# Attention and LoRA block on one core: queries of 23 of 32 pairs by seven products of halves, block transfers over three issuing queues, masks of the expert map built later

## The chip, the cores and the metric

The kernel runs on one core of a Trainium2 chip. A core has a matrix engine (PE, with its weight loads shown as PEld), a vector engine (DVE), a scalar engine (ACT), a general engine (POOL) and a queue engine that only issues transfers (SP). All work on a shared on-chip memory (SBUF); PE writes into a small accumulation memory (PSUM) of eight banks, which DVE and ACT can read. Transfers are issued by SP, ACT or POOL and wait in the issuing engine's own order. The metric is the device time of one execution in microseconds, as the median of several runs.

## The reference

The input x has 1024 rows of 512 features, in float32 throughout. With LN for a layer norm without weights, the block computes

```
h   = LN(x)
q   = h @ w_q   (32 heads of 128)      k, v = h @ w_k, h @ w_v   (8 heads of 128)
a   = softmax(causal(q k^T / sqrt(128))) v         four query heads share one k, v head
x   = x + LN(a @ w_o)
h   = LN(x)
y   = h @ base_W^T + base_b + 2 * sum_e (h A_e^T * weight_e) B_e^T
out = x + LN(y)
```

The weights of the experts come from a router: a softmax over 15 logits, the top eight of them, and `expert_map`, which says to which of eight experts each of the 15 belongs.

## The kernel before

The 1024 rows are eight tiles of 128 rows, t = 0 to 7. A group g is one of the eight k, v heads with its four query heads. A **block** is one (g, t): the attention of 128 rows for four heads. Two blocks with neighbouring t form a **pair** (g, u), whose queries are projected together, 256 rows at a time. There are 64 blocks and 32 pairs; groups 0 to 5 run one after the other with t rising, groups 6 and 7 are interleaved at the end, in pairs, and there the second half (router, base product, LoRA) follows each finished tile.

A loop over the blocks (`for i in range(N)`, L804) issues everything. In each block i four **score** steps run, each for 32 rows of all four heads (L403): PE multiplies the queries with all keys up to there (one or two matmuls of at most 512 columns, with the queries as weights), DVE adds the causal mask and takes the maximum (L420, L422), ACT takes the exponential with its sum (L427), and a step later ACT divides by the sum (L434) and DVE transposes 32 x 32 squares into the tile T (L440). POOL clears the part of the row behind the diagonal (`memset`, L425). Two score tiles in PSUM alternate. When T is full, sixteen transfers (`to_keys`, L452) move its 32-row squares to their places in the tile K, which is what the next product needs. K and T have one buffer each for even and for odd t.

Between the scores, `run_share` spreads the rest of the block's PE work over its four quarters by column count. That work is a list, made anew for every block:

- in odd blocks `q`, the query projection of the next pair (`project_q`, L330): four heads, each a sum over four chunks of 128 features, 16 matmuls of 256 columns; two heads share a PSUM bank and ACT copies each bank out, scaled by 1/sqrt(128) (L343);
- `pv`, the product of v and K for the block two earlier (`weighted_values`, tile `po`, L462), t + 1 matmuls of 512 columns; ACT copies its result to `attnT` (L468);
- in even blocks `o_pair`, the output projection of a pair four blocks back (`project_o_pair`, L510). It is already done by seven products of halves: sums of the operands (`sums`, on DVE, L519 to L522; of the weights on POOL, `combine_o`, L505), products pa to pf, and accumulations by DVE (L543);
- projections of k and v, and later the router and the base product.

The order is `then = begins[:1] + q + ends[:-1] + rest[:4] + ...` (L821): in an odd block all the queries come first and the weighted values after them. A float32 matmul runs as two passes on PE, each with its own weight load, so the trace has two rows for each.

What is kept in program order and what is not: instructions wrapped in `keep` stay in written order on their engine; the others are placed by a scheduler. Matmuls, transfers and most score work are kept. PSUM has four banks for the two score tiles, three for a rotating tag `pm` that all projections share, and one for `po`. The query weights of a group, two tiles of 512 KB, have one buffer each and are loaded by ACT's queue at the start of the last but one block of the group before (`load_q`, L120, L724).

For blocks 3 to 62, `to_keys` issues all sixteen transfers from SP (`alone`, L447); for the first three and the last, two of three come from SP and the third from POOL. At block 8 `prepare_ffn` (L199) lets POOL load the second half's small weights and the expert map, and DVE turns the map into eight masks (L208 to L214), which the router uses from block 55 on or so.

Of the kernel before, what the change touches and what calls it, by code (L numbers as in the profile page):

```python
# [15 lines left out]
P = 128  # L16
# [6 lines left out]
def kernel(  # L23
# [28 lines left out]

    nc = tc.nc
    S, H = x.shape
    D = P
# [30 lines left out]
    blocks = [(g, 2 * u + e) for g, u in pairs for e in range(2)]  # L88
    N = len(blocks)
    N2 = (G - 2) * NT  # L90

    def keep(ins):
        return tc.keep_in_program_order(ins)
# [11 lines left out]
    def load(dst, src, by=nc.sync):  # L105
        keep(by.dma_start(dst, src))  # L106
# [13 lines left out]
    def load_q(g, i, by=nc.scalar):  # L120

        if weights.get(("q", i), (None,))[0] == g:
            return
        hw = R * D // 2
        w = wp.tile([P, KC, hw], F32, tag=f"wq{i}", name=f"wq_{g}_{i}", bufs=1)
        load(w, w_q[:, ts(2 * g + i, hw)].rearrange("(c p) n -> p c n", p=P), by)
        weights["q", i] = (g, w)

    def load_v(gv, i, by=nc.scalar):

# [66 lines left out]
            keep(nc.vector.tensor_copy(smask[ts(h, SQ), :], mask[ts(h, SQ), ts(h, SQ)]))  # L197

    def prepare_ffn():  # L199

        load(ra_sb[:, :, :NR], router_wt.rearrange("(c p) n -> p c n", p=P), nc.gpsimd)
        load(ra_sb[:, :, NR:], a_t.rearrange("(c p) n -> p c n", p=P), nc.gpsimd)
        load(bt_sb, b_t, nc.gpsimd)
        load(bias_bc, base_b.partition_broadcast(P), nc.gpsimd)
        load(rb_bc, router_b.partition_broadcast(P), nc.gpsimd)
        load(emap_i, expert_map.partition_broadcast(P), nc.gpsimd)
        emap_f = const.tile([P, NR], F32, tag="emap_f", name="emap_f")
# [110 lines left out]
    def project_k(g, qb):  # L318
        def finish(pm):
            kT = kTs[g, qb] = act.tile([P, QB], F32, tag="kT", name=f"kT_{g}_{qb}", bufs=2 * NQB)  # L320
            nc.scalar.copy(kT, pm)

        def term(c):
            return weights["k", g][:, c, :], xnT[qb][:, c, :]

        return chained(
            lambda: bank(f"pk_{g}_{qb}"), [lambda c=c: term(c) for c in range(KC)], finish
        )

    def project_q(g, u):  # L330

        pm = {}

        def get(j):
            if j % 2 == 0:
                pm[0] = bank(f"pq_{g}_{u}_{j}")
            return pm[0][:, ts(j % 2, PQ)]

        def finish(j):
            if j == 0:  # L340
                qTs[g, u] = act.tile([P, PQ // SQ, R, SQ], F32, tag="qT", name=f"qT_{g}_{u}")
            if j % 2:
                nc.scalar.mul(  # L343
                    qTs[g, u][:, :, j - 1 : j + 1, :].rearrange("p s h q -> p h s q"),
                    pm[0].rearrange("p (h s q) -> p h s q", h=2, q=SQ),
                    scale,
                )

        def term(j, c):
            w = weights["q", j // 2]  # L350
            assert w[0] == g
            rhs = xnT[u * PQ // QB][:, c, ts(u % (QB // PQ), PQ)]
            return w[1][:, c, ts(j % 2, D)], rhs
# [9 lines left out]
        return work  # L363

    turned, keyed = {}, {}

# [36 lines left out]
    def scores(g, t, j):  # L403

        n = t * P + (j + 1) * SQ
        full = (t + 1) * P
        name = f"{g}_{t}_{j}"
        s = ps_s.tile([P, S], F32, tag="s", name=f"s_{name}")
        for c0 in range(0, n, QB):
            w = min(QB, n - c0)  # L410
            matmul(
                s[:, c0 : c0 + w],
                qTs[g, t // 2][:, (t % 2) * NSUB + j, :, :].rearrange("p h q -> p (h q)"),
                kTs[g, c0 // QB][:, :w],
                start=True,
                stop=True,
            )
# [12 lines left out]

        def rescale():
            rec = small.tile([P, 1], F32, tag="rec", name=f"rec_{name}")
            keep(nc.vector.reciprocal(rec, total))  # L433
            keep(nc.scalar.mul(p[:, :n], p[:, :n], rec))  # L434

        def finish():
            if j == 0:
                turned[g, t] = turn_view(turn_tile("T", g, t), t)
            pin(
                nc.vector.transpose(  # L440
                    turned[g, t][:, :, j, :, :].rearrange("p b k q -> p k b q"),
                    p[:, :full].rearrange("p (k b q) -> p k b q", b=R, q=SQ),
                )
            )
            if j == NSUB - 1:
                three = (nc.sync, nc.sync, nc.gpsimd)
                alone = 3 <= blocks.index((g, t)) < N - 1  # L447
                to_keys(g, t, by=three[:1] if alone else three)

        score_tile["rescale"], score_tile["finish"] = rescale, finish  # L450

    def to_keys(g, t, by=(nc.sync,)):  # L452

        src = turned.pop((g, t))
        dst = keyed[g, t] = turn_view(turn_tile("K", g, t), t)
        for h in range(R):
            for b in range(NSUB):
                load(dst[ts(b, SQ), h], src[ts(h, SQ), b], by[(h * NSUB + b) % len(by)])
# [227 lines left out]
    def projections(i):  # L686


        g, t = blocks[i]
        q, other = [], []  # L690
        m = i // 2 + 1
        if i == 0:
            later["q"] = project_q(*pairs[m])
            q = later["q"][: 2 * KC]
        elif i == 1:
            q = later["q"][2 * KC :]
        elif i % 2 and m < len(pairs):
            q = project_q(*pairs[m])
        if i < N2:
            if t == 2:  # L700
                other += project_k(g, 1)
            if t == 6:
                other += project_k(g + 1, 0)
            if g == 0 and t < 2:
                other += [(P * KC, lambda n=TPB + 2 + t: input_turn(n))]
                other += project_v(0, 2 + t)
            elif g % GV == 0 and (g or t >= TPB):
                other += project_v(g // GV, t)
        else:
# [94 lines left out]
    for i in range(N):  # L804
# [13 lines left out]
            begins = ffn_router(t)  # L818

        rest = o + weave(o_pair, other + pv[:2] + begins[1:] + pv[2:])  # L820
        then = begins[:1] + q + ends[:-1] + rest[:4] + ends[-1:] + rest[4:]  # L821
        for n in range(NSUB):
            scores(*blocks[i], n)
            run_share(then, n, NSUB)
        if i == 1:
            combine_o(0)
        if i == NT:
            prepare_ffn()
        ready += complete(i, 7, 8)
        for t in [t for t in ready if ("done", t) in state]:  # L830
            ready.remove(t)
# [81 lines left out]
```

## Time and profile before

| what | value |
|---|---|
| three runs | 1087.78, 1087.92, 1088.68 us (median 1087.92) |
| the profiled execution | 1087.64 us |
| its span, first to last instruction | 1085.9 us |
| mean granted PE clock | 0.996 |
| busy: PE, PEld, DVE, ACT, POOL | 98%, 65%, 60%, 45%, 11% |
| query projection on PE | 1024 rows |
| transfers K<-T | 1004 from SP, 20 from POOL |

A row of the profile reads: line of the kernel, engine, operation, tile written <- tiles read, shape, count; then busy time, mean duration of one in ns, and idle time of the engine before it with what ended that. Matmuls overlap in the pipeline, so the distance between starts tells their pace and not their duration. In a timeline row the first number is the start and the second the length of what was merged, in microseconds from the start of the span. Tile names carry no buffer numbers: `pq` is the PSUM tile of the queries, `s` a score tile, `po` that of the weighted values.

### The profile page before, as it was taken

Reading aid. Unit: us, or ns where it says so; the run is one execution under the profiler, and the core shown is the slowest. Engines: PE = TensorE matmul, PEld = TensorE weight load, DVE = VectorE, ACT = ScalarE, POOL = GpSimd, SP = SyncE. Lnnn points to the kernel's source line nnn. Section 1 sums busy time; section 2 is a strip of 40 time slices with the busy share of each in tenths; the row PEclk is TensorE's granted clock in tenths of the full one; section 3 lists DMA queues with packets and bytes.
Section 4 is the critical chain, followed back from the end, with each engine's and each line's share of the span. In section 5 each row is a group of like instructions: output and inputs, shape, how many; then the busy total and the mean of one; then the engine's idle time right before and its main releaser. Section 6 shows DMA issues by size and latency. Waiting matters only on the chain.

```text
span 1085.9 us, 12864 instructions
## 1 busy us (share of the span) xinstructions
PE 1068.1 (98%) x3846; PEld 705.7 (65%) x3846; DVE 652.6 (60%) x1528; ACT 492.3 (45%) x992; POOL 115.0 (11%) x300
## 2 busy tenths in 40 slices
PE   8999999999999999999999999999999999999986
PEld 7776666666676666666676666666777566466443
DVE  4566546665465555765456555665346766576747
ACT  2654535554345434544345444555335554453511
POOL 2500012000110002000020001100020110111212
PEclk9999999999999999999999999999999999999998
DMA  5244352554135432455125441464333755544221
GB/s 184 62 107 124 68 119 63 160 137 92 36 71 158 92 85 52 121 140 117 39 65 142 103 108 42 105 169 115 88 104 101 170 132 124 131 104 103 71 78 39
DMA packets 79061, 111.82 MB, mean 103 GB/s; under 512 B 18176, under 2 KB 50560, under 8 KB 78992
## 3 DMA queue, kind: packets, MB, share of 16 engines
q1 hardware_dynamic: 52976, 82.08, 32.0%
q10 hardware_dynamic: 25040, 27.27, 7.9%
q0 software_dynamic: 976, 1.65, 0.7%
q8 instruction: 31, 0.51, 0.2%
q14 instruction: 38, 0.31, 0.1%
HBM read 33.34 MB, written 2.10 MB: 33 GB/s over the span
## 4 chain that ended last, share of the span: by engine, by line
PE 87%; DVE 5%; ACT 2%; DMA 2%; SPq 1%; POOL 1%; issue 1%; POOLq 0%; ACTq 0%; DVEq 0%
PE po L100 21%; PE s L100 19%; PE pq L100 18%; PE pk L100 5%; PE pv L100 4%; PE pe L100 4%; PE pa L100 4%; PE pO L100 2%; PE pc L100 2%; PE pb L100 2%; PE pd L100 2%; PE pf L100 2%; DVE T L440 1%; SPq L106 1%; DVE nmax L422 1%; ACT p L427 1%
## 5 line engine op out<-in xcount | busy, mean ns | idle before, releaser
L100 PE MATMUL po<-K,v 128*128 128x512 f32 x576 | 277.4, 596 | 6.2 <-DMA K<-T 4.6
L100 PE MATMUL s<-kT,qT 128*128 128x512 f32 (+15 forms) x768 | 271.8, 463 | 0.0
L427 ACT ACTIVATE p<-s,nmax 128x32 f32<-128x32 f32 (+31 forms) x256 | 179.2, 700 | 198.3 <-DVE nmax L422 192.2
L434 ACT ACTIVATE p<-p,rec 128x32 f32<-128x32 f32 (+31 forms) x256 | 187.9, 734 | 178.1 <-DVE rec L433 121.2
L440 DVE STREAM_TRANSPOSE T<-p 128x128 f32<-128x128 f32 (+7 forms) x256 | 198.4, 775 | 103.1 <-ACT p L434 88.9
L100 PE MATMUL pq<-xnT,wq 128*128 128x256 f32 x1024 | 235.7, 379 | 0.0
L100 PEld LDWEIGHTS s<-kT,qT 128*128 128x128 f32 x768 | 145.6, 190 | 122.1 <-issue 108.1
L100 PEld LDWEIGHTS pq<-xnT,wq 128*128 128x128 f32 x1024 | 192.8, 190 | 38.5 <-issue 16.5
L422 DVE TENSOR_REDUCE nmax<-s 128x1 f32<-128x32 f32 (+31 forms) x256 | 180.7, 706 | 8.3
L100 PEld LDWEIGHTS po<-K,v 128*128 128x128 f32 x576 | 107.7, 191 | 80.3 <-issue 63.8
L420 DVE TENSOR_TENSOR s<-s,smask 128x32 f32<-128x32 f32 x256 | 47.6, 186 | 124.9 <-PE s L100 124.3
L425 POOL MEMSET p<- 128x96 f32 (+2 forms) x192 | 29.8, 156 | 842.7 <-DVE T L440 775.4
L433 DVE RECIPROCAL rec<-total 128x1 f32<-128x1 f32 x256 | 39.8, 155 | 51.9 <-ACT p L427 49.7
L100 PE MATMUL pv<-wv,xnT 128*128 128x256 f32 x256 | 67.3, 380 | 0.4 <-ACT xnT L255 0.4
L343 ACT ACTIVATE qT<-pq 128x512 f32<-128x512 f32 x64 | 38.1, 595 | 65.3 <-PE pq L100 65.2
L468 ACT COPY attnT<-po 128x512 f32<-128x512 f32 x64 | 37.3, 583 | 61.5 <-PE po L100 61.3
L100 PE MATMUL pk<-xnT,wk 128*128 128x512 f32 x128 | 64.5, 593 | 0.0
L100 PE MATMUL pa<-wo,attnT 128*128 128x256 f32 x224 | 62.7, 390 | 0.0
L100 PEld LDWEIGHTS pa<-wo,attnT 128*128 128x128 f32 x224 | 41.8, 193 | 19.8 <-issue 14.8
L100 PEld LDWEIGHTS pv<-wv,xnT 128*128 128x128 f32 x256 | 48.0, 190 | 9.9 <-issue 2.7
L427 ACT ACTIVATION_READ_ACCUMULATOR p<-s,nmax 128x1 f32 x256 | 49.5, 193 | 0.0
L519 DVE TENSOR_TENSOR sums<-attnT 128x256 f32<-128x256 f32 x28 | 11.9, 424 | 56.5 <-ACT attnT L468 56.4
(107 smaller groups left out, 779.4 us busy)
## 6 DMA issues: line engine op xcount, KB each, us to landing
K<-T SPq DMA_DIRECT2D x128, 128.0 KB, 2.4
K<-T SPq DMA_DIRECT2D x128, 112.0 KB, 2.2
wq<-in_w_q_dram ACTq DMA_DIRECT2D x27, 512.0 KB, 4.8
K<-T SPq DMA_DIRECT2D x128, 96.0 KB, 2.2
K<-T SPq DMA_DIRECT2D x128, 80.0 KB, 2.1
K<-T SPq DMA_DIRECT2D x123, 64.0 KB, 2.0
wo<-in_w_o_dram ACTq DMA_DIRECT2D x28, 256.0 KB, 4.0
K<-T SPq DMA_DIRECT2D x123, 48.0 KB, 1.9
```

The lines of the kernel that those rows point to most:

```text
L100: keep(nc.tensor.matmul(*args, **kw))
L106: keep(by.dma_start(dst, src))
L343: nc.scalar.mul(qTs[g, u][:, :, j - 1 : j + 1, :].rearrange("p s h q -> p h s q"), pm[0].rearrange("p (h s q) -> p h s q", h=2, q=SQ), scale,)
L420: keep(nc.vector.tensor_tensor(s[:, n - SQ : n], s[:, n - SQ : n], smask, ALU.add))
L422: keep(nc.vector.tensor_reduce(nmax, s[:, :n], AX.X, ALU.max, negate=True))
L425: nc.gpsimd.memset(p[:, n:full], 0.0)
L427: keep(nc.scalar.activation(p[:, :n], s[:, :n], AF.Exp, bias=nmax, accum_out=total))
L433: keep(nc.vector.reciprocal(rec, total))
L434: keep(nc.scalar.mul(p[:, :n], p[:, :n], rec))
L440: nc.vector.transpose(turned[g, t][:, :, j, :, :].rearrange("p b k q -> p k b q"), p[:, :full].rearrange("p (k b q) -> p k b q", b=R, q=SQ),)
L468: copy = nc.scalar.copy(o, po)
L519: nc.vector.tensor_tensor(s1, a21, a22, ALU.add)
```

## The change

For pairs 2 to 24 (`QW`), the query projection is done by seven products of halves. Two of the four heads stand against the other two in the weights (`a11`, `a12` and `a21`, `a22`: heads 0, 1 and 2, 3; first and second half of the features), the two tiles of the pair against each other in the rows (`b11` to `b22`). POOL forms sums of weights once per group (`combine_q`: three new tiles and one in place, 512 elements each) and differences of the normed input once per pair (`combine_x`: four of 256 elements). PE then runs seven products, each for two heads and two chunks, 28 matmuls of 128 columns. The results fill four PSUM banks. One ACT copy writes the first product to both heads of one tile, and seven DVE additions of 256 elements put the rest together (`merge`). The scale goes from the query copy to the key copy. All blocks, no longer only the first three and the last, issue K's transfers from SP, SP and POOL in turn. The masks of the expert map are made at block 12 instead of 8. In odd blocks with t > 1 from block 5 on, the queries are woven with the first three fifths of the other work; what is left of it follows them.

```diff
+    QW = range(2, N2 // 2 + 1)
...
+    def combine_q(m):
...
+        w = [weights["q", i][1] for i in range(2)]
+        hk = KC // 2
+        a11, a12, a21, a22 = w[0][:, :hk], w[0][:, hk:], w[1][:, :hk], w[1][:, hk:]
+        s1, s2, s4 = (
+            ffn.tile([P, hk, 2 * D], F32, tag="hy", name=f"sq_{g}_{n}", bufs=3) for n in range(3)
+        )
+        for dst, p, q, op in (
+            (s1, a21, a22, ALU.add),
+            (s2, s1, a11, ALU.subtract),
+            (a21, a11, a21, ALU.subtract),
+            (s4, a12, s2, ALU.subtract),
+        ):
+            keep(nc.gpsimd.tensor_tensor(dst, p, q, op))
+        weights["sq", 0] = (a11, a12, s4, a22, s1, s2, a21)
...
+    def combine_x(m):
...
+        xp = xnT[u * PQ // QB][:, :, ts(u % (QB // PQ), PQ)]
+        b11, b12, b21, b22 = xp[:, :hk, :P], xp[:, :hk, P:], xp[:, hk:, :P], xp[:, hk:, P:]
+        t12, t34 = (ffn.tile([P, 2, hk, P], F32, tag="x", name=f"tx_{m}_{n}") for n in range(2))
+        t1, t2, t3, t4 = t12[:, 0], t12[:, 1], t34[:, 0], t34[:, 1]
+        for dst, p, q in ((t1, b12, b11), (t2, b22, t1), (t3, b22, b12), (t4, b21, t2)):
+            nc.gpsimd.tensor_tensor(dst, p, q, ALU.subtract)
+        weights["tx"] = (b11, b21, b22, t4, t1, t2, t3)
...
-            nc.scalar.copy(kT, pm)
+            nc.scalar.mul(kT, pm, scale)
...
-                nc.scalar.mul(
+                nc.scalar.copy(
                     qTs[g, u][:, :, j - 1 : j + 1, :].rearrange("p s h q -> p h s q"),
                     pm[0].rearrange("p (h s q) -> p h s q", h=2, q=SQ),
-                    scale,
                 )
...
+    def project_q_halves(m):
...
+        def add(dst, src, to):
+            nc.vector.tensor_tensor(dst, src, to, ALU.add)
+
+        def merge(b):
+
+            one, two = pm[b][:, 0], pm[b][:, 1]
+            if b == 0:
+                nc.scalar.copy(both(0), one.unsqueeze(1).to_broadcast([P, 2, NSUB, 2 * SQ]))
+                add(half(0, 0), two, half(0, 0))
+            elif b == 1:
+                add(half(1, 0), one, half(0, 1))
+                add(half(0, 1), two, half(1, 0))
+            elif b == 2:
+                add(half(1, 1), one, half(0, 1))
+                add(half(1, 0), one, half(1, 0))
+                add(half(1, 0), two, half(1, 0))
+            else:
+                add(half(0, 1), one, half(0, 1))
+
+        order = (0, 1, 5, 6, 4, 2, 3)
+
+        def piece(n, c, k):
+            i, b, x = order[n], n // 2, n % 2
...
+            matmul(
+                pm[b][:, x, :, ts(c, SQ)],
+                weights["sq", 0][i][:, k, ts(c, D)],
+                weights["tx"][i][:, k, :].rearrange("p (s q) -> p s q", q=SQ),
+                start=(k == 0),
+                stop=(k == hk - 1),
+            )
+            if c == 1 and k == hk - 1 and (x == 1 or n == 6):
+                merge(b)
...
-                three = (nc.sync, nc.sync, nc.gpsimd)
-                alone = 3 <= blocks.index((g, t)) < N - 1
-                to_keys(g, t, by=three[:1] if alone else three)
+                to_keys(g, t)
...
-    def to_keys(g, t, by=(nc.sync,)):
+    def to_keys(g, t, by=(nc.sync, nc.sync, nc.gpsimd)):
...
-            q = project_q(*pairs[m])
+            q = project_q_halves(m) if m in QW else project_q(*pairs[m])
...
+        if i % 2 and i // 2 + 1 in QW and blocks[i][1] > 1 and i > 3:
+            cut = len(rest) * 3 // 5
+            q, rest = weave(q, rest[:cut]), rest[cut:]
         then = begins[:1] + q + ends[:-1] + rest[:4] + ends[-1:] + rest[4:]
         for n in range(NSUB):
             scores(*blocks[i], n)
             run_share(then, n, NSUB)
+            if i % 2 == 0 and n < 2 and i // 2 + 1 in QW:
+                (combine_x, combine_q)[n](i // 2 + 1)
...
+        if i == NT + 4:
+            prepare_map()
```

`prepare_map` holds the lines of `prepare_ffn` that turn the map into masks, unchanged.

More of the change, by code (lines that the diff above doesn't have):

```diff
@@ L127, in load_q @@
         weights["q", i] = (g, w)
+    def combine_q(m):
+        g = pairs[m][0]
+        if weights.get("sq", (None,))[0] == g:
+            return
+        w = [weights["q", i][1] for i in range(2)]
[12 more added lines that the diff above has]
+        weights["sq", 0] = (a11, a12, s4, a22, s1, s2, a21)
+        weights["sq"] = (g,)
+    def combine_x(m):
+        u = pairs[m][1]
+        hk = KC // 2
+        xp = xnT[u * PQ // QB][:, :, ts(u % (QB // PQ), PQ)]
[5 more added lines that the diff above has]
+        weights["tx"] = (b11, b21, b22, t4, t1, t2, t3)
     def load_v(gv, i, by=nc.scalar):
@@ L206, in prepare_ffn, with prepare_map @@
         load(emap_i, expert_map.partition_broadcast(P), nc.gpsimd)
+    def prepare_map():
         emap_f = const.tile([P, NR], F32, tag="emap_f", name="emap_f")
@@ L363, in project_q, with half, both @@
         return work
+    def project_q_halves(m):
+        g, u = pairs[m]
+        hk = KC // 2
+        pm = {}
+        def half(e, h):
+            return both(e)[:, h]
+        def both(e):
+            q = qTs[g, u][:, ts(e, NSUB), :, :]
+            return q.rearrange("p s (x h) q -> p x s (h q)", x=2)
+        def add(dst, src, to):
[17 more added lines that the diff above has]
+            i, b, x = order[n], n // 2, n % 2
+            if n == c == k == 0:
+                qTs[g, u] = act.tile([P, PQ // SQ, R, SQ], F32, tag="qT", name=f"qT_{g}_{u}")
+            if x == c == k == 0:
+                whole = bank(f"pq_{g}_{u}_{b}")
+                pm[b] = whole.rearrange("p (x s n) -> p x s n", x=2, s=NSUB)
+            assert weights["sq"] == (g,)
+            matmul(
[7 more added lines that the diff above has]
+                merge(b)
+        return [
+            (P, lambda n=n, c=c, k=k: piece(n, c, k))
+            for n in range(7)
+            for c in range(2)
+            for k in range(hk)
+        ]
     turned, keyed = {}, {}
```

## The prediction

> **What bounds the kernel now.** First the page's engine rows, then the waits of PE.
>
> ```profile
> span 1085.9 us, 12864 instructions
> ...
> PE 1068.1 (98%) x3846; PEld 705.7 (65%) x3846; DVE 652.6 (60%) x1528; ACT 492.3 (45%) x992; POOL 115.0 (11%) x300
> ...
> L100 PE MATMUL pq<-xnT,wq 128*128 128x256 f32 x1024 | 235.7, 379 | 0.0
> ```
> ```profile
> PE po L100 <- DMA K<-T: 4.6, 1, 4.6
> ```
>
> PE is full from start to end and waits about 10 us in all, 4.6 of it once, near the end. So PE's own pace sets the end, and a matmul's price is the distance to the next start, not its duration (ends are modelled). Each matmul here is two passes: 512 query matmuls, 1024 rows. The timeline gives the pace:
>
> ```profile
> 24.01 1.04 PE L103 MATMUL ptx_x<-ident,K_x 128*128 128x128 f32 x8
> 24.88 0.39 PE L100 MATMUL s<-kT,qT 128*128 128x32 f32 x2
> 25.11 1.54 PE L100 MATMUL pq<-xnT,wq 128*128 128x256 f32 x6
> ...
> 29.52 0.39 PE L100 MATMUL s<-kT,qT 128*128 128x128 f32 x2
> 29.75 1.89 PE L100 MATMUL pv<-wv,xnT 128*128 128x256 f32 x8
> ```
> ```profile
> 679.61 2.32 PE L100 MATMUL pq<-xnT,wq 128*128 128x256 f32 x10
> 681.76 0.97 PE L100 MATMUL s<-kT,qT 128*128 128x480 f32 x2
> ```
>
> Ten 256-column passes take 2.15 us, 0.215 each. A 128-column pass takes (24.88-24.01)/8 = 0.109 as a transpose and 0.23/2 = 0.115 (rounded starts) as a score. A 32-column pass also takes 0.115: below 128 columns something else than columns sets the pace, the next weight load. Next, whether DVE has room, in group 3's blocks t = 3, 4, 5 (window; length; PE, PEld, DVE, ACT, POOL busy; clock; DMA), and Pool's prices:
>
> ```profile
> 424.18:435.92 11.74, 11.74 (x46) 8.36 (x44) 6.72 (x17) 6.10 (x13) 5.48 (x7) 1.00 0.34 89
> 435.92:448.86 12.94, 12.94 (x51) 8.82 (x50) 10.68 (x25) 6.80 (x13) 0.30 (x2) 1.00 0.29 69
> 448.86:464.04 15.18, 15.18 (x57) 10.48 (x56) 9.78 (x18) 8.40 (x15) 0.61 (x4) 1.00 0.66 173
> ```
> ```profile
> L505 POOL TENSOR_TENSOR wot<-wo 128x512 f32<-128x512 f32 x14 | 17.8, 1273 | 8.5 <-PE pe L100 8.0
> ...
> L106 POOL DMA_DIRECT2D K<-T x20 | 10.1, 511 | 10.5 <-DVE shift_y L237 6.3 <-DMA K<-T 2.5 <-DVE T L440 1.5
> ```
>
> Last, the chain at the one long wait: SP issues the 16 transfers of K for the last block but one, 0.63 us apart, and PE stands until they land.
>
> ```profile
> 1032.39 0.59 SPq L106
> 1033.03 1.91 DMA K<-T
> 1034.94 0.23 issue
> 1035.16 1.77 PE po L100 x2
> ```
>
> **What the Trainium skill says.** "TensorE: Matmul & The Clock Gate", section LDWEIGHTS, prices a load by its columns, P/1.2 ns: 107 ns for 128. The page's PEld rows say 190 each, but starts lie 0.11 apart in the stretch above, so loads overlap and the section agrees with the pace. The same page, section HAM oscillation, says that a long idle of PE halves its clock: after the 4.6 us wait two 512-column passes take 1.56 us (0.86 elsewhere). "DMA: Bandwidth & Descriptors", section Issuing engines are not separate DMA queues: more issuers save only issue time; the chain shows that issue time. "SBUF — State Buffer", section SBUF: two separate sides: a Pool instruction and a DVE one with two SBUF inputs shut each other out. The merges read PSUM, so only the four `sums` of a pair (0.42 each) can meet Pool; no lock is visible in this trace.
>
> **The change, part by part.**
>
> *Query products.* Before, 16 matmuls of 256 columns in two passes: 32 x 0.215 = 6.88 us of PE per pair. After, 7 products x 2 heads x 2 chunks = 28 matmuls of 128 columns, 56 passes. Bounds of a pass: 0.109 (columns) and 0.115 (load, rounded up); I take 0.111. 56 x 0.111 = 6.22, gain 0.66 (0.44 to 0.78); 23 pairs: 15.2 us (10.1 to 17.9). One thing isn't in the trace: the output is written in four pieces of 32 columns, each 64 apart. The moving operand of `po` is read in such pieces at 0.43 per 512 columns, like `pk`, so pieces cost nothing on the read side; I take nothing for the write, and bound it under rival C.
>
> *Merges.* Two ACT copies of 0.595 become one; seven DVE additions of 256 PSUM elements come. Accumulations of 512 and 768 elements take 0.68 and 0.94, so 256 take 0.42: 2.9 us per odd block. Block t = 3 shrinks to 11.1 with DVE at 6.72 + 2.9 = 9.6; t = 5 to 14.5 with 12.7; block t = 4 has 10.7 of 12.9. It fits, but a tight stretch. Cover of the last merge: what PE still does after the queries, two fifths of the rest: one `po` (0.86) at t = 3 in odd groups, two at t = 5, three at t = 7, all eight at t = 1. Behind the last product come a merge (0.42 plus some 0.2 of hand-over), so only t = 3 can show: a DVE busy with a 0.7 transpose makes the next block's first score late by up to 0.5. Uncovered everywhere it would cost 0.6 x 23 = 14 us. I take 1.5 us in all (0 to 6). PSUM: four banks a pair from three buffers; the fourth needs the first's merge, done some 3 us before. Nothing.
>
> *Pool sums.* `combine_x`: four of 256 elements, half of 1.27, 0.65 each, 2.6 us per pair; `combine_q`: 4 x 1.27 = 5.1 us per group in block t = 6, waiting for the weights (landing 4.8 us after issue). Both have over half a block; Pool goes from 115 us to 115 + 23 x 2.6 + 7 x 5.1 + K's share below = some 365 of 1070. In t = 6 K's Pool transfers stand behind the sums: 6.5 (weights) + 5.1 + 5 x 0.51 + 2.3 landing = 16.5 us into a 19.5 us block, and `po` wants them 2.7 us into the next. Nothing, with 5 us of room. In the first group three jobs meet: `combine_o` (5.1 until 41.1), then the sums (until 46.3), then K of block 1, which lands some 5 us later than now; `po` wants it at 55, but the transpose of block 3, which needs that transfer done at 49.9, slips by about 1: DVE has it to spare.
>
> *K's transfers.* In 60 blocks SP issues 11 instead of 16: 6.9 us instead of 10.1; Pool five in 2.6. The trace has Pool issue only transfers of 16 to 64 KB, at 0.50 to 0.55 each whatever the size; I take that for 128 KB too, and at double it Pool's five (5.1) still end before SP's eleven. K is complete 3.2 us earlier. In most blocks nobody waited for it, so no gain by itself; but the new weave starts `po` 2.7 us into blocks t = 5 instead of after all queries. There the first `po` comes after a score (2 x 0.43 + 2 x 0.136) and seven query matmuls (7 x 2 x 0.111): 2.7 us. K of t = 3 is transposed 4.6 us into block 4 (group 1: block from 183.44, transpose until 188.02); +6.9 + 2.2 = 13.7, wanted at 12.9 + 2.7 = 15.6: hidden, while 16 on SP would be 16.9 and late. At the end of the kernel the wait of 4.6 shrinks by up to 3.2 and the half clock (0.7 + 0.85 lost on the next six passes) may not come: up to 4.7. Against it: in the changed order the last block's transpose stands behind the merges of pa and pb, some 2 us later, and the next `po` then waits for that K. I take 3.0 (1 to 4.4).
>
> *Map masks.* DVE's 4.1 us wait for the map goes; no PE wait hangs on it (its waits name none): 0. *Scale* on the key copy instead of the query copy: same two kinds of ACT instruction (0.58 and 0.6): 0.
>
> Sum on the profiled execution, 1087.64 (span 1085.9 and 1.7 around it): -15.2 - 3.0 + 1.5 = -16.7, 1070.9. The median of the runs is 0.3 above it: 1071.2. I say 1071.
>
> **The rivals.** *B: DVE hands over too late.* Merges stand in DVE's order between score work, and block t = 4 is 83% busy. If each odd block loses 0.4 us at the next score, 9 us go: 1080. For: the 0.86 cover, Pool's sums meeting `sums`. Against: two score buffers, and DVE spends 124 us of its idle time waiting for PE's scores. *C: slower.* The 128-column pass. The gain vanishes at 6.88/56 = 0.123 per pass, 12 ns above my value; with the 3.0 of the end, at 0.125. A write that costs 3 to 4 ns a piece would do it, or loads that do not overlap in long runs: at PEld's 0.19, 56 x 0.19 = 10.6 per pair, +86 us, 1172. At 0.13 per pass: +9.2 - 3.0 + 1.5, 1095. Against: eight 0.109 passes with eight loads; but the trace has no long run of 128-column products with new weights. *D: Pool late.* It issues in order, and in blocks 48 to 63 its transfers share the queue with the powers that the norms wait for: 2.6 us of delay against about 4 us of room per step. If half of 16 blocks lost 1 us of PE: 1079. *E: the three queues help nobody*, and the end keeps its wait: 1074, inside the main case.
>
> **How the numbers follow.** Main case with E 0.70 (1064 to 1077), B 0.14, D 0.06, C 0.10. The main case's ends: 0.109 a pass, no stall and 4.4 at the end give 1087.9 - 17.9 - 4.4 = 1065.6; 0.113, 4 us of stalls and 2 at the end give 1087.9 - 12.7 + 4 - 2 = 1077. For 8 in 10 I go up to B and D, 1064 to 1082. What tells from no change is 0.2%, 2.2 us. Faster: main, D and most of B, 0.89; within, 0.03; slower, C and a little of B, 0.08.
>
> **What would show it.** Right: 9 x 32 = 288 rows of `pq` at 256 columns and 23 x 56 = 1288 at 128, starts 0.109 to 0.115 apart; block t = 3 near 11.1 us, t = 7 near 18; DVE near 720 us; PE's wait for K at the end 1 to 2 us. Wrong: passes over 0.12 apart (C), PE rows that wait for DVE `qT` (B), for `K` or `wq` sums from Pool (D).

## The result and the profile after

The changed kernel takes 1078.1 us (median of 4 runs, 1077.82 to 1079.19) against 1087.87 us for the kernel before (1087.78 to 1088.68): a ratio of 0.991, with a 95% interval of 0.9893 to 0.9928. It is 9.8 us faster, not 16.7, which was the sum of the prediction. The profiled execution took 1077.89 us, 9.75 less than its counterpart before. In what follows, blocks have the numbers 0 to 63 in the order of the loop.

The page of the changed kernel: the engine rows and the new merges.

```profile
PE 1053.7 (98%) x4398; PEld 708.9 (66%) x4398; DVE 703.5 (65%) x1689; ACT 480.9 (45%) x969; POOL 360.7 (34%) x720
...
L418 DVE TENSOR_TENSOR qT<-pq,qT 128x256 f32<-128x256 f32 x161 | 63.4, 413 | 34.8 <-ACT qT L424 27.2
```

PE is as full as before, and Pool works three times as long. The waits of PE (us in total, times, longest):

```profile
PE s L102 <- ACT attnT L565: 2.1, 3, 0.7
PE po L102 <- DMA K<-T: 2.1, 2, 1.9
...
PE pl L102 <- ACT hT L293: 1.4, 1, 1.4
PE s L102 <- DVE qT L418: 1.2, 4, 0.7
```

The wait for K near the end has gone from 4.6 to 1.9 us. In its place PE's scores (`s`) now wait seven times, 3.3 us in all, and `pl` waits 1.4 us. The windows of t = 3 and 4 of group 3 (window; length; PE, PEld, DVE, ACT, POOL busy; clock; DMA), the same blocks as in the prediction:

```profile
417.75:429.70 11.95, 11.24 (x69) 8.37 (x68) 8.88 (x24) 6.98 (x15) 10.51 (x16) 1.00 0.36 90
429.70:442.73 13.03, 13.03 (x51) 8.96 (x52) 11.45 (x25) 6.32 (x13) 3.01 (x10) 1.00 0.32 81
```

PE is busy for 11.24 us in the first, as the prediction's 11.1 would have it, but the block lasts 11.95. PE stands at its end. The timeline of PE there:

```profile
424.43 1.06 PE L102 MATMUL pq<-tx,sq 128*128 128x128 f32 x8
425.32 0.83 PE L102 MATMUL pq<-xnT,sq 128*128 128x128 f32 x6
...
427.97 1.02 PE L102 MATMUL po<-K,v 128*128 128x512 f32 x2
429.70 1.24 PE L102 MATMUL s<-kT,qT 128*128 128x512 f32 x4 [0.71 <-ACT attnT L565]
```

And of DVE in the same stretch:

```profile
427.62 0.68 DVE L521 TENSOR_REDUCE nmax<-s 128x1 f32<-128x512 f32 x1
428.22 0.70 DVE L539 STREAM_TRANSPOSE T<-p 128x512 f32<-128x512 f32 x1
428.84 1.05 DVE L418 TENSOR_TENSOR qT<-pq,qT 128x256 f32<-128x256 f32 x3
```

Eight passes of the products take 425.32 - 424.43 = 0.89 us, 0.111 each. The last product is through at 427.97, but DVE does a maximum and a transpose of 512 columns first, so three merges run from 428.84 to 429.9, and the first score of the next block, which reads what they write, starts at 429.70. One `po` (0.86 us) was the only cover: the only work of PE that is left while the merges run. The page names the copy `attnT` as the releaser, but the score doesn't read it. The score starts 0.15 us after the end of the second of the three merges. At the end of t = 5, where no such copy stands near, it starts at the same distance behind the last merge; so it is the merge that holds it.

Where the 9.8 us come from, measured from span to span: the start of the first score, the start of the last block, the last start of a PE instruction, the end of the span.

| part | predicted | measured |
|---|---|---|
| run-in to the first score (24.70 to 25.23 us over all kernels of this study) | 0 | +0.26 |
| products, 23 pairs | -15.2 | -15.1 (0.65 to 0.66 in every odd block without a stall) |
| stalls elsewhere in blocks 0 to 62, net | +1.5 | +3.6 |
| last block, from its first score to the last PE start | -3.0 | -1.75 (56.21 to 54.46) |
| from the last PE start to the end of the span | 0 | +3.2 (8.60 to 11.83) |
| sum | -16.7 | -9.8 |

The last part is not in the prediction at all. What grew there is one instruction of Pool's sequencer, which the profile doesn't count as busy and calls DRAIN. Its rows (count; min/median/max in ns; first and last start), of the kernel before:

```profile
L909 POOLq DRAIN  x3: 46/102/3117, 1080.5 to 1085.6; - x3
```

and of the changed one:

```profile
L1014 POOLq DRAIN  x3: 46/102/7852, 1067.4 to 1075.8; - x3
```

Each kernel ends with a DRAIN on SP, ACT, DVE and Pool. Pool's longest lasts 3.12 us before, and SP's stores of the last rows outlast it; it lasts 7.85 us after, and 0.8 us after its end the span is over. Pool issued 26 transfers before and 326 after.

### The profile page after: what moved, and what is told of

It reads as the page before. It is cut to its first block, busy times and chain, and to the rows that moved or that the text cites. A ratio compares the mean times of both kernels' runs of the same rounds, so it can differ in the third digit from the quotient of the medians.

```text
span 1076.1 us, 15090 instructions
## 1 busy us (share of the span) xinstructions
PE 1053.7 (98%) x4398; PEld 708.9 (66%) x4398; DVE 703.5 (65%) x1689; ACT 480.9 (45%) x969; POOL 360.7 (34%) x720
## 4 chain that ended last, share of the span: by engine, by line
PE 89%; DVE 5%; POOL 2%; DMA 1%; ACT 1%; issue 1%; SPq 1%; POOLq 0%; ACTq 0%; DVEq 0%
PE po L102 21%; PE s L102 21%; PE pq L102 17%; PE pv L102 5%; PE pk L102 5%; PE pa L102 4%; PE pe L102 4%; PE pO L102 2%; PE pb L102 2%; PE pd L102 2%; PE pc L102 2%; PE pf L102 2%; SPq L108 1%; DVE T L539 1%; POOL K L108 1%
## 5 line engine op out<-in xcount | busy, mean ns | idle before, releaser
L108 POOL DMA_DIRECT2D K<-T x320 | 157.9, 500 | 265.0 <-DVE s L519 55.1
L102 PEld LDWEIGHTS s<-kT,qT 128*128 128x128 f32 x768 | 141.4, 190 | 127.1 <-issue 107.2
L102 PEld LDWEIGHTS po<-K,v 128*128 128x128 f32 x576 | 104.8, 190 | 64.3 <-issue 54.1
L102 PE MATMUL pq<-xnT,wq 128*128 128x128 f32 (+1 forms) x656 | 113.8, 321 | 0.0
L102 PEld LDWEIGHTS pq<-xnT,wq 128*128 128x128 f32 x656 | 100.6, 191 | 14.7 <-issue 7.7
L418 DVE TENSOR_TENSOR qT<-pq,qT 128x256 f32<-128x256 f32 x161 | 63.4, 413 | 34.8 <-ACT qT L424 27.2
L102 PE MATMUL pv<-wv,xnT 128*128 128x256 f32 x256 | 71.2, 381 | 0.5 <-ACT xnT L293 0.5
L162 POOL TENSOR_TENSOR tx<-xnT 128x256 f32<-128x256 f32 x46 | 33.4, 726 | 81.1 <-PE pq L102 74.3
L102 PEld LDWEIGHTS pq<-tx,wq 128*128 128x128 f32 x368 | 49.6, 192 | 9.1 <-issue 7.7
L102 PEld LDWEIGHTS pq<-tx,sq 128*128 128x128 f32 x368 | 49.8, 192 | 8.6 <-issue 8.3
```

The lines of the kernel that those rows point to most:

```text
L102: keep(nc.tensor.matmul(*args, **kw))
L162: nc.gpsimd.tensor_tensor(dst, p, q, ALU.subtract)
L418: nc.vector.tensor_tensor(dst, src, to, ALU.add)
```

## The experiments

Each diff is against the kernel named in the heading. Times are medians, with the ratio to the kernel before on the same chip where there is an interval. Lengths of blocks and waits come from the one profiled execution of each kernel.

**K by SP alone, in the changed kernel (e1_sp_alone).**

```diff
-                to_keys(g, t)
+                three = (nc.sync, nc.sync, nc.gpsimd)
+                alone = 3 <= blocks.index((g, t)) < N - 1
+                to_keys(g, t, by=three[:1] if alone else three)
```

> The changed kernel, with the transfers of K of blocks 3 to 62 issued by SP alone again, as before. Theory (the transfers that Pool issues cost time at the very end: Pool's closing DRAIN took 7.85 us in the changed kernel and 3.12 us before, and the 300 more transfers are what differs): the DRAIN falls to about 3.1 us and what lies between the last addition of DVE and the end of the span from 6.4 to 3.2 us, a gain of 3.2. Against it PE's wait for K near the end comes back (4.6 us, with the half clock after it): a loss of 1.8 to 4.7. By the prediction's step on K, po in blocks t = 5 of odd groups would now wait some 1.3 us three times, 3.9 in all. Sum 1076.5 to 1083. Rival (the DRAIN has another reason): the DRAIN stays at 7.8 and only the losses count, 1080 to 1087.

Measured: 1081.96 us, ratio 0.9954 (0.9938 to 0.9971), so some 4 us slower than the changed kernel. Pool's DRAIN is 3.11 us and the end from the last PE start is 8.6 us, as before. The wait for K near the end is back at 5.0 us, and blocks t = 5 of groups 1, 3, 5 are 1.56, 1.11 and 0.97 us longer than in the changed kernel, 3.6 in all. The timeline of PE in the first of them:

```profile
196.89 1.72 PE L102 MATMUL pq<-xnT,wq 128*128 128x128 f32 x14
199.94 1.10 PE L102 MATMUL po<-K,v 128*128 128x512 f32 x2 [1.32 <-DMA wo<-in_w_o_dram]
```

After seven query matmuls (14 passes) `po` waits 1.32 us, as the prediction worked out for SP alone; in groups 3 and 5 it waits 0.87 and 0.73. The page names the load of `wo`, which landed last before `po` could start, but the two kernels differ only in who issues K, and without the change of issuers that wait is not there. So in the changed kernel the three queues are needed for the weave at t = 5; they save PE there and near the end, and pay part of it back at the DRAIN.

**The three queues alone, in the kernel before (e2_three_only).**

```diff
-                alone = 3 <= blocks.index((g, t)) < N - 1
+                alone = False
```

> The kernel before, with nothing changed but that K of every block is issued by SP, SP and Pool in turn. The prediction's step: 3.0 us less (1 to 4.4), all of it at the wait for K near the end, 1083.5 to 1087. Theory of the DRAIN: the wait near the end goes (3 to 4.7 us less), Pool's closing DRAIN grows from 3.1 to 7.8 us and 3.2 us more lie behind the last addition: 1086.4 to 1088.1, the same as before within what can be told.

Measured: 1089.81 us, ratio 1.0035 (1.0021 to 1.0049). By themselves the three queues make the kernel slower. The DRAIN takes 7.86 us and adds 3.2 us to the end; the last block is 1.72 us shorter, no more, though the merges are not there; block 12 gains 0.66, where K of t = 2 had come just too late; block 9 loses 0.78. At the end of block 8 `prepare_ffn` lets Pool issue its six loads, and they now stand behind Pool's five transfers of K. The expert map is the last of them, and DVE waits for it in its order. The waits of DVE in this kernel:

```profile
DVE emap_f L208 <- DMA emap_i<-in_expert_map_dram: 6.0, 1, 6.0
```

In the kernel before that wait is 4.1 us, and no wait of PE hangs on it. Here a score of block 9 waits 0.66 us for ACT's exponential, which stands behind DVE's maximum, which stands behind the masks. The change moves the masks to block 12, where DVE doesn't wait for the map any more.

**The queries first at t = 3 and 5 (e3_cover, against the changed kernel).**

```diff
-        if i % 2 and i // 2 + 1 in QW and blocks[i][1] > 1 and i > 3:
+        if i % 2 and i // 2 + 1 in QW and blocks[i][1] > 5:
```

> The changed kernel, with the query products of blocks t = 3 and t = 5 not woven with the rest but ahead of it, so that at t = 3 of odd groups two po and at t = 5 five po (instead of one and two) stand between the last product and the next block's first score. Theory (the merges are late because the cover is short): t = 3 of odd groups falls from 11.96 to about 11.1 us, t = 5 from 14.87 to 14.5, three of each: 3.7 us less, and up to 1.5 less in block 3 of the first group, 1073 to 1074.5. Rival (DVE is too full around block t = 4, cover or not): the wait only moves to another score or to a product that waits for its bank, and less than 1 us is won, 1077 to 1078.

Measured: 1073.54 us, ratio 0.988 (0.9865 to 0.9894); the span is 4.6 us shorter. All six blocks now gain their full 0.65 us, and the blocks behind them (12, 14, 28, 30, 44 and 46), which had lost 0.07 to 0.08 each, lose nothing: 4.1 us. The other 0.5 lie in block 9, which the edit leaves alone. Its `po` waits for K, and this wait differs between kernels that do the same work there: 0.24 us in the changed kernel, none here. The end of t = 3 in group 3:

```profile
425.23 1.88 PE L102 MATMUL po<-K,v 128*128 128x512 f32 x4
426.95 1.02 PE L102 MATMUL s<-kT,qT 128*128 128x512 f32 x2
```

Two `po` in a row, and the score starts without a wait. DVE is as busy as before (11.46 of 12.94 us in the following block). So it was the cover, not the load on DVE. Block 3 of the first group is untouched by this (+0.84 us against the kernel before, +0.87 in the changed one): that loss has another cause.

**Small transfers by Pool, in the kernel before (e4_tiny, e6_tiny_half, e10_rows).** The first issues 300 transfers of 4 bytes, the second stops at block 32:

```diff
     for i in range(N):
         loads(i)
+        if 3 <= i < N - 1:
+            for n in range(5):
+                k = 5 * (i - 3) + n
+                load(scratch[ts(k // 3, 1), ts(k % 3, 1)], base_b[:1].unsqueeze(0), nc.gpsimd)
```

the third issues 60 of 128 rows each (one run each of the last two):

```diff
+        if 3 <= i < 63:
+            load(scratch[:, ts(i - 3, 1)], x[:P, :1], nc.gpsimd)
```

> The kernel before, with 300 transfers of 4 bytes into a scratch tile, issued by Pool, five at the start of each of the blocks 3 to 62; K's transfers stay on SP. If Pool's closing DRAIN grows with the number of transfers that Pool has issued: 7.8 us instead of 3.1, and 3.2 us more at the end, 1091. If it grows with bytes or with the packets that a transfer is cut into (9.5 thousand in the changed kernel, 300 here): it stays near 3.1 to 3.3 and the time at 1088.

> The kernel before with 150 transfers of 4 bytes issued by Pool instead of 300, five in each of the blocks 3 to 32. With 15.8 ns for each Pool transfer the closing DRAIN takes 3.12 + 150 x 0.0158 = 5.5 us. If it has two levels only (few, many): 3.1 or 7.86.

> The kernel before with 60 transfers issued by Pool, each of 128 rows of 4 bytes (one in each of the blocks 3 to 62). The 4-byte transfers of e4_tiny left 32 packets each in the record, as K's transfers did, so number and packets haven't been told apart. By number: the DRAIN takes 3.12 + 60 x 0.0158 = 4.1 us. By packets (0.49 ns each, from 4.74 us for 9.6 thousand): about 6.9 us if each of the 128 rows counts as one or more.

Measured: 1090.8 us, ratio 1.0037 (1.0024 to 1.005); 1088.93 us; 1093.16 us. The DRAIN rows, of the 300:

```profile
L914 POOLq DRAIN  x3: 46/102/7856, 1081.5 to 1089.9; - x3
```

and of the 60 with 128 rows:

```profile
L912 POOLq DRAIN  x3: 46/102/8021, 1082.6 to 1091.1; - x3
```

300 transfers of 4 bytes give the same DRAIN as 300 K transfers of 16 to 128 KB, to 4 ns: bytes don't matter. 150 give 5.48 us, in line with 15.8 ns each (4.74 us more for 300). But 60 transfers give 8.02 us: neither 4.1 (by number) nor, with the 1920 packets that they add to the record, the 4.1 that 0.49 ns a packet would give. The 6.9 that I had written down for packets rested on 7680 of them. Both theories fall.

**Cover and fewer Pool transfers (e7_cover_few, against e3_cover).**

```diff
-                to_keys(g, t)
+                three = (nc.sync, nc.sync, nc.gpsimd)
+                alone = 3 <= blocks.index((g, t)) < N - 2
+                to_keys(g, t, by=three[:1] if alone else three)
```

> The changed kernel with the longer cover of e3_cover at t = 3 and 5, and with Pool issuing K transfers only for the first three blocks and the last two; SP alone for the others. Theory: K isn't late at t = 5 any more, because there po follows all query products; the DRAIN falls to 3.2 us (3.1 and five more transfers); the wait for K near the end stays at 1.9. e3_cover's 1073.5 less 3.2, and less 0.25 in two blocks of the last groups where Pool's transfers stood before the norms' powers: 1070. Rival (K by SP alone is late at t = 5 or elsewhere all the same): 0.5 to 1.5 us in each of three to six blocks come back, 1072 to 1076.

Measured: 1072.95 us, ratio 0.987 (0.9855 to 0.9884), between the two theories. The end is 8.4 us, 3.4 shorter than in e3_cover, and t = 5 has no wait any more. But t = 4 of groups 1, 3, 5 lost 1.48, 0.62 and 1.57 us: there `po` is early and wants K of t = 2, which sixteen transfers of SP bring too late now that t = 3 is shorter. And the last block took 55.88 us instead of 54.49: the long wait of `po` in it is 2.5 us instead of 1.9, and PE's clock fell to half for 3.4 us after it (see the end of this document). The profiled execution was the slowest of the four, 2.2 us above the median. The DRAIN took 3.53 us: five transfers more than before, and 0.41 us more.

**The products for pairs 3 to 26 (e8_later, against e7_cover_few).**

```diff
-    QW = range(2, N2 // 2 + 1)
+    QW = range(3, N2 // 2 + 3)
```

> e7_cover_few, with the seven products for the queries of pairs 3 to 26 instead of 2 to 24. Theory: block 3 of the first group lost 1.5 us because Pool's sums for pair 2 stood before the memset that its exp waits for; with the old products for pair 2 that block takes its old 11.74 us (0.85 less than now), and each of the two further pairs gives 0.66: 2.2 us less than e7_cover_few, 1068. Rival (pair 3's sums only move the jam to a later block, or the sums of pairs 25 and 26 meet Pool's other work): some 1 us less, or none.

Measured: 1070.13 us, ratio 0.9844 (0.9828 to 0.9861), the fastest kernel of the study. The two further pairs give 0.66 each. But blocks 2 to 4 lose 1.03, 0.10 and 0.62 us against the kernel before: the token sums of pair 3 (`combine_x`, not kept in order) were placed right behind `combine_o`, ahead of the memsets. So the jam moved, as the rival says. The larger part of the gain in the profiled executions (5.3 us, against 2.8 between the medians) lies in a last block of 53.63 us instead of 55.88, where this time the clock didn't fall, and in t = 4 of groups 1 and 5, 1.1 us less each; this edit doesn't touch either.

**All of it joined (e9_joined, against e8_later).**

```diff
-                alone = 3 <= blocks.index((g, t)) < N - 2
-                to_keys(g, t, by=three[:1] if alone else three)
+                i = blocks.index((g, t))
+                some = i < 3 or i >= N - 4 or (i < N2 and g % 2 and t == 2)
+                to_keys(g, t, by=three if some else three[:1])
...
-            nc.gpsimd.tensor_tensor(dst, p, q, ALU.subtract)
+            keep(nc.gpsimd.tensor_tensor(dst, p, q, ALU.subtract))
```

> What the runs so far point to, joined: the longer cover at t = 3 and 5; the seven products for pairs 3 to 26; the sums of the token halves kept at their place in Pool's program, so that they don't stand before the memsets of block 2; three queues only for K of the first three blocks, of block t = 2 in the odd groups (where e7_cover_few lost 0.6 to 1.5 us of PE three times in block t = 4) and of the last four blocks, where e7_cover_few had K of the last block but one behind sixteen transfers on SP. Theory: against e8_later 1.7 us less in blocks 2 to 4, 1.5 less in t = 4, 0.4 more at the DRAIN (56 Pool transfers), and at the end 0 to 0.9 more (1.7 won there instead of 2.6): 1067 to 1068. Rival (the order of Pool's program isn't what delayed blocks 2 to 4): 1069 to 1070.

Measured: 1072.34 us, ratio 0.9856 (0.984 to 0.9873): no better than e8_later. Blocks 2 and 3 are at their old times and t = 4 of the odd groups loses nothing, as expected; but block 4 loses 1.73 us (`pc` waits 1.5 us behind DVE), block 9 takes 0.9 us longer than in e8_later (its `po` waits 0.64 us for K), the last block takes 55.52 us, with 3.4 us at half clock, and the DRAIN takes 5.57 us, not 3.6: 30 transfers more than before, 2.46 us more, 82 ns each, as in e7_cover_few (5, 0.41) and e10_rows (60, 4.90).

**Another number of Pool transfers, and another order in the first group (e11_count, e12_order).** Against e3_cover:

```diff
-    QW = range(2, N2 // 2 + 1)
+    QW = range(2, N2 // 2 + 3)
...
-                to_keys(g, t)
+                three = (nc.sync, nc.sync, nc.gpsimd)
+                to_keys(g, t, by=three[:1] if g in (2, 4) else three)
```

and e12_order on top:

```diff
         if i == 1:
+            combine_q(2)
+        if i == 3:
             combine_o(0)
```

> e3_cover, with the seven products for pairs 2 to 26, and with K of the groups 2 and 4 issued by SP alone, so that Pool issues 246 transfers instead of 326. All DRAINs so far fit 0.985 us + 0.0818 us x (number of Pool's transfers modulo 121): 26 gives 3.11, 31 gives 3.52, 56 gives 5.57, 86 gives 8.02, 176 and 326 leave 55 and 84 and give 5.48 and 7.86. 246 leaves 4: a DRAIN of 1.31 us, and the 3.2 us that the changed kernel has more at its end go. With 0.66 for each of two more pairs: 1073.5 - 3.2 - 1.3 = 1069. Rival (the DRAIN grows by 15.8 ns a transfer): 3.11 + 220 x 0.0158 = 6.6 us, of which about 2 lie on the path: 1071.

> e11_count, with Pool's work of the first group in another order: the sums of the weights for pair 2 at the end of block 1, where combine_o stood, and combine_o at the end of block 3. Theory (in the changed kernel block 3 of the first group lost 1.5 us because K's transfers and a memset stood behind combine_o and these sums together, 10.2 us): block 3 falls from 12.58 to about 11.1 us and K of block 1 is issued at its old time, 1.5 us less than e11_count, 1067.5. Rival (as in e9_joined the jam moves into block 4, where pb waits for combine_o): nothing won, or 1 us lost.

Measured: 1077.34 us, ratio 0.9904 (0.9887 to 0.992), and 1074.54 us, ratio 0.9879 (0.9864 to 0.9894). The DRAIN of e11_count:

```profile
L1015 POOLq DRAIN  x3: 46/102/10908, 1063.8 to 1075.2; - x3
```

10.9 us, where 1.31 was expected, and where the 15.8 ns law gives 6.6. It began 0.29 us later after PE's last start than in the other kernels, so that it ended where one of 11.2 us would have. All seven numbers of transfers in one table, with 0.985 us + 0.0818 us x k:

| transfers issued by Pool | 26 | 31 | 56 | 86 | 176 | 246 | 326 |
|---|---|---|---|---|---|---|---|
| DRAIN, us | 3.12 | 3.52 | 5.57 | 8.02 | 5.48 | 10.91 | 7.86 |
| k that fits | 26 | 31 | 56 | 86 | 55 | 121 (125 with the 0.29) | 84 |
| transfers - k | 0 | 0 | 0 | 0 | 121 | 125 (121) | 242 |

The first four give the price: 82 ns for each transfer that Pool has issued. The other three read as if 121 at a time had been cleared before the end, once at 176 and 246, twice at 326. This is a reading of the lengths alone, made after they were known; no row of the traces shows a clearing. If it holds, what I had wrong is the moment: at 246 the second one hasn't come.

The first group was the surer gain. Pool and DVE around block 3 in the changed kernel, where block 3 begins at 45.30; Pool's timeline:

```profile
46.49 2.47 POOL L108 DMA_DIRECT2D K<-T  x5
48.95 0.25 POOL L524 MEMSET p<- 128x32 f32 x2
```

DVE's:

```profile
49.13 0.58 DVE L539 STREAM_TRANSPOSE T<-p 128x384 f32<-128x384 f32 x1 [3.69 <-POOL p L524]
```

and Pool's in e12_order:

```profile
41.21 2.47 POOL L108 DMA_DIRECT2D K<-T  x5
43.67 0.47 POOL L524 MEMSET p<- 128x32 f32 x2
```

With `combine_o` out of the way, K and the memsets are 5.3 us earlier. Block 3 takes 11.08 us instead of 12.59 in e11_count. The span is 2.0 us shorter, 2.8 by the medians; the other 0.5 of the 2.0 lie in block 9, whose wait for K differs as much where nothing was changed.

**Half the columns in every second pass (e5_half_columns, against the changed kernel).**

```diff
-                pm[b][:, x, :, ts(c, SQ)],
+                pm[b][:, x, : NSUB >> k, ts(c, SQ)],
...
-                weights["tx"][i][:, k, :].rearrange("p (s q) -> p s q", q=SQ),
+                weights["tx"][i][:, k, : P >> k].rearrange("p (s q) -> p s q", q=SQ),
```

> The changed kernel, where the second of the two chunks of each of the 28 query products moves only 64 columns and writes only 64 of the 128 (it leaves a quarter of the products' work out). If the next weight load sets the pace below 128 columns, as the prediction took it: both kinds of pass start 0.111 us apart, and the time stays at 1078. If the columns set it: 0.055 for the half ones, 28 x 0.055 x 23 = 35 us less, 1043.

Measured: 1075.81 us (one run); the 2 us less lie in block 3 (0.85) and in t = 5 of the odd groups (1.0), where the changed kernel has its stalls. The odd blocks without stalls are as long as in the changed kernel to 0.01 us, with a quarter of the moved columns gone; starts are 0.11 us apart on average: 0.165 from one 128-column pass to the next, 0.058 from one 64-column pass to the next, 0.112 where the width changes. It isn't the columns that set the pace at 128 and below. The weight loads of the same passes keep an even step:

```profile
451.55 0.64 PEld L102 LDWEIGHTS pq<-xnT,sq 128*128 128x128 f32 x5 [0.24 <-issue]
452.10 0.30 PEld L102 LDWEIGHTS pq<-tx,wq 128*128 128x128 f32 x2
```

Five loads start in 452.10 - 451.55 = 0.55 us, 0.110 each. Where load follows load in these products, nine in ten starts are 0.110 to 0.113 us apart, here as in the changed kernel. So it is the loads that set the pace.

## Why the prediction was right and where it was not

1078.1 us lies in the stated range of 1064 to 1082, but outside the main case (1064 to 1077). The range had been drawn out for rivals B and D. B is part of what came (the merges, 3.7 us), but the largest single miss, the DRAIN, is in no rival; so that the range held is in part luck.

**Query products: right.** 0.111 to 0.112 us per pass, 0.65 to 0.66 us per pair, 15.1 us. The write in four pieces costs nothing that can be seen. Half of the columns less in every second pass changes nothing, and the loads start 0.11 us apart all the same: they are the floor, as the prediction took it. Rival C is out.

**Merges and their cover: the mechanism right, the size wrong.** A merge takes 0.413 us (0.42 predicted). "Only t = 3 can show", by up to 0.5, was the failed step. It counted one merge, a hand-over and at worst a transpose of 0.7 us behind the last product; DVE had a maximum of 0.68 as well, and three merges, two of which the score needed. Measured: 0.87 us at t = 3 of the odd groups, and 0.34 at t = 5, where the prediction had nothing and a maximum of 0.96 and a transpose of 0.97 us stand in front of the last merge; 3.7 us in six blocks. e3_cover gives them all back. Rival B had the right place and the wrong spread: 15 of 23 blocks lost nothing, block 9 lost 0.1, and block 3 for another reason, which comes next. DVE's 703.5 us were to be 720; nothing hangs on it.

**Pool's sums: wrong in the first group.** The sum of 256 elements takes 0.727 us, not 0.65, and of 512 elements 1.27, as predicted; at steady state nothing waits for them. But the step by which the transpose "slips by about 1: DVE has it to spare" failed: 1.5 us are lost in block 3. The prediction saw `combine_o`, the sums and K in one row on Pool, but left out the memset behind them. DVE's transpose of block 2 waits 3.69 us for that, and DVE's later work with it. e12_order shows that the order on Pool is the cause: K and the memset move together there, and the trace names the memset.

**K's transfers: right where they are hidden.** e1_sp_alone finds the wait of 1.3 us at t = 5 that the prediction worked out for SP alone. Not foreseen: block 12, where K had been late before, gains 0.6, and at t = 0 of groups 1, 3 and 5 `po`'s wait for the copy of `attnT` (1.1 us in three times before) is gone, 0.6 a block. The three queues are not needed for either: e1_sp_alone, with the new queries and SP alone, has both gains. e2_three_only, with the queues and the old queries, has only that of block 12. These 2.5 us, set against 6.1 lost (1.5 in block 3, 3.7 in six blocks, 0.5 at the blocks that follow them, and small ones), make the net 3.6 of the table. Rival E falls: the three queues are needed, at t = 5 with this weave and at the end; taken alone they cost more than they give.

**The end: half.** The wait went from 4.6 to 1.9 us (1 to 2 predicted). Up to the pass before `pb` the last block is 4.5 us ahead of the kernel before, near the 4.7 that the prediction had as the most: 2.8 by the wait and 1.7 by the half clock that doesn't come. Then 2.8 us are lost again. The last block's transpose does stand behind the merges of pa and pb, but the next `po` waits only 0.32 us for it; `pb` waits 0.30 and `pl` 1.36. PE, DVE (two views) in the changed kernel:

```profile
1024.22 1.13 PE L102 MATMUL pb<-wot,sums 128*128 128x256 f32 x4 [0.30 <-DVE acc L640]
...
1028.43 1.25 PE L102 MATMUL pl<-ra_sb,hT 128*128 128x143 f32 x8 [1.36 <-ACT hT L293]
```
```profile
1025.39 0.96 DVE L640 TENSOR_TENSOR acc<-pb,acc 128x768 f32<-128x768 f32 x1 [0.96 <-PE pb L102]
1026.26 0.70 DVE L539 STREAM_TRANSPOSE T<-p 128x512 f32<-128x512 f32 x1
1026.89 0.17 DVE L275 TENSOR_SCALAR shift_y<-mv_y,rstd_y 128x1 f32<-128x1 f32 x1
```

Behind the transpose stands `shift_y`; ACT's norm waits for that, the copy `hT` stands behind the norm on ACT, and `pl` waits for the copy. Before, all this ran while PE stood waiting for K. So a stall that is cut uncovers the chain that it hid. The gain is 1.75, and 1.72 in e2_three_only, where no query product is changed.

**The closing DRAIN: missing.** 3.2 us, nearly half of the 7 that the prediction is off; the term stood at nothing because it was not asked for. Pool's 300 further issues were priced at 0.50 each on Pool and followed to their landing; that they could cost anything after the last instruction was not asked. The row was there in the trace of before (3.12 us, overlapped by the last stores), and no line of waits or groups names it.

**The masks and the scale** were not tried alone; e2_three_only shows what the masks would cost at block 8 beside the three queues. D (Pool late) shows as 0.25 us in blocks 50 and 56, which e1_sp_alone doesn't lose.

## What to carry to other kernels

Count what an engine issues to the end of the program, not only to the landing of its transfers: hundreds of Pool-issued transfers can leave a clean-up of several microseconds behind the last useful instruction, so give Pool only those that somebody waits for. When work moves onto an in-order engine, price the last instruction's place in that order, behind every maximum, transpose and memset, and not its duration; then ask what covers it. And when a stall is shortened, look for the chains that ran in its shadow.

## What the runs showed of the hardware

- Pool's closing DRAIN takes 0.99 us and 82 ns for each transfer that Pool issued (26 to 86 of them), whatever the size (4 bytes or 128 KB) or rows (1 or 128). At 176, 246 and 326 it is shorter than that, as if 121 or 242 had been cleared before. It sets the end of these kernels where it takes over some 4.5 us, an estimate: the end is 8.4 to 8.6 us with the short ones, less 3.2 before the DRAIN begins and 0.8 behind it.
- The half clock of PE after a wait isn't a matter of the wait's length alone. The Trainium skill, "TensorE: Matmul & The Clock Gate", section HAM oscillation, speaks of idle gaps over about 3.4 us; here a wait of 1.9 us was enough in one kernel and not in another. In all 14 traces the granted clock changes only at whole multiples of 3.413 us from its first record, and where half speed comes before the end of the kernel, it lasts one or two such steps. So it matters how a wait falls on these steps. The step with the wait in the changed kernel, then that of e11_count and the one behind it (window; length, PE busy; clock; DMA):

```profile
1019.35:1022.77 3.42, 1.67 (x6) 1.00 0.13 31
1013.14:1016.55 3.41, 1.51 (x6) 1.00 0.18 43
1016.55:1019.97 3.42, 3.42 (x8) 0.50 0.00 0
```

The waits are 1.88 and 1.90 us. In e11_count the whole wait lies in one step; in the changed kernel its first 0.13 us fall in the step before, PE is busy for 1.67 us of the step, and the clock stays. The limit between the two was not measured closer. In the kernel before half speed lasts one step, in e4_tiny, with the same PE order and a wait as long, two: 1.3 us more, in the profiled execution of 1091.96 us. In e7_cover_few and e9_joined one step of half speed falls in the last block, which is 1.4 and 1.1 us longer than in the changed kernel. That of e8_later has none; it is 0.8 us shorter than in the changed kernel, for the most part because three waits in it are 0.7 us shorter together.

- e8_later, at 0.9844 of the kernel before, beats both kernels. A kernel with e12_order's first group and few Pool transfers was not run.
